# Softmax of the cross attention: one exponential for eight heads instead of eight

## The chip, the cores and the metric

The kernel runs on one core of a Trainium2 chip. The time is the device time of one launch, in microseconds (us). Before the change it is 1782.53 us, the median of three runs (1781.92 to 1785.18).

A core has five engines that run side by side, each with its own queue in order: TensorE (PE; PEld is its loading of weights), VectorE (DVE), ScalarE (ACT), GpSimd (POOL) and SyncE (SP, which only issues transfers here). TensorE writes to PSUM, the other engines compute from PSUM or SBUF; POOL works in SBUF alone. In the profile an instruction stands under the line of the kernel that issued it (L359 is line 359).

## The reference

The program is a decoder of two layers on an input of 16 x 128 x 256 floats (16 sequences of 128 tokens of 256 numbers), each block followed by a layer norm: an attention with a causal mask, a gated ensemble, a mixture of experts, then an attention with a band mask, a cross attention with a second input `ctx_512`, and again experts. The change touches the cross attention of the second layer alone, which has 16 heads of 16 numbers and no mask:

```
qh = (q @ Wq + bq).reshape(B, LQ, HEADS, D_K).transpose(0, 2, 1, 3)
kh = (k @ Wk + bk).reshape(B, LKV, HEADS, D_K).transpose(0, 2, 1, 3)
scores = jnp.einsum('bhqd,bhkd->bhqk', qh, kh) * scale
attn = jax.nn.softmax(scores, axis=-1)
out = jnp.einsum('bhqk,bhkd->bhqd', attn, vh)
```

So for every sequence and head there are 128 x 128 scores, and each row of 128 keys is turned into weights: the row's maximum is subtracted, the exponential taken, and the result divided by its sum.

## The kernel before

**Tiles and stages.** The 16 sequences are worked on in four groups of four. A group passes through the six blocks in order; each block is a Python generator that issues a few instructions and then yields an estimate of the time they take. A small weaver merges two such streams into one program: attention blocks as the main stream, and the dense blocks (ensemble and experts) of other groups as the side stream, by given ratios. So while one group's cross attention runs, matrix products of another group's dense block run in between. For the four groups the merging ends in these calls: cross attention (block 4) of group 0 and of group 1 each behind its own band attention (block 3), and groups 2 and 3 in one stretch, each beside the dense stream.

**The order on the engines.** The program's order is not quite that of the queues. The framework below places the instructions of each engine by their order in the text among those that it reckons ready, from its own estimates of durations; a few places are fixed by hand (`together`, `joined`, `keep_in_program_order`).

**Cross attention.** `cross1` projects queries, keys and values, then calls `attention16`, which the band attention calls too. It goes through eight units, one for each sequence of the group and each half of the heads (eight heads a unit). For a unit:

1. POOL writes the keys of four heads side by side, masked by head (`kb`, L493).
2. TensorE makes the scores of eight heads, 128 x 1024 numbers, in two banks of PSUM (tile `psS`, four matmuls of 64 rows, issued through L52). `psS` has one buffer, so the next unit's scores can't be written before all readers of this one are done.
3. `softmax`. For the attentions with a mask, DVE first copies the scores to SBUF with the mask (L349, tile `e`); the cross attention has no mask, `seen` is `None`, and the scores stay in PSUM. DVE reduces each row to its negated maximum (L354, `nmax`, eight numbers a row). ACT then runs one exponential a head, with that maximum as its bias, and gives the row's total with it (L359; the total is a second record, ACTIVATION_READ_ACCUMULATOR). DVE takes the reciprocal of the totals (L364), and POOL multiplies the weights by it (L365).
4. Two units later TensorE transposes the weights (L57, into `psO`), ACT copies them to SBUF (L374, `eT`), TensorE multiplies them with the values (L52), ACT and DVE pick the heads' rows (L528, L531), and the output product is added to the input (L290) and normed.

**The dense work beside it.** Beside group 0's cross attention runs the ensemble: TensorE's hidden rows are finished by DVE (L803). Beside groups 2 and 3 run the experts of the second layer, whose hidden rows are finished by ACT with Gelu (L1213); Gelu and the exponential lie in different function tables, so ACT loads a table (ACT_TABLE_LOAD) at each change between them. Beside group 1 the routed experts of the first layer end, with gathers from memory whose results DVE adds (L292), and the second layer's experts begin. In these dense blocks DVE also builds sums of the hidden rows (L687 to L690) and adds products to accumulators (L709, L711).

Of the kernel before, what the change touches and what calls it, by code (L numbers as in the profile page):

```python
# [10 lines left out]
AF = mybir.ActivationFunctionType  # L11
ALU = mybir.AluOpType
AX = mybir.AxisListType

P = 128
# [14 lines left out]
def kernel(ctx: ExitStack, tc: tile.TileContext, a: dict, out: bass.AP):  # L30
    nc = tc.nc
# [311 lines left out]
    def softmax(s, seen):  # L343

        n = 2 * s.shape[2]
        e = p3.tile([P, n, P], F32, tag="p", name="e")
        scores = e.rearrange("p (s h) k -> p s h k", s=2)
        if seen is not None:
            nc.vector.tensor_tensor(  # L349
                scores, s, seen.unsqueeze(1).unsqueeze(1).to_broadcast([P, 2, n // 2, P]), ALU.min  # L350
            )
            s = scores
        nmax = sp.tile([P, n], F32, tag="nmax", name="nmax")
        nc.vector.tensor_reduce(  # L354
            nmax.rearrange("p (s h) -> p s h", s=2), s, AX.X, ALU.max, negate=True
        )
        total = sp.tile([P, n], F32, tag="total", name="total")
        for h in range(n):
            nc.scalar.activation(  # L359
                e[:, h, :], s[:, h // (n // 2), h % (n // 2), :],  # L360
                AF.Exp, bias=nmax[:, h:h + 1], accum_out=total[:, h:h + 1],
            )
        inv = sp.tile([P, n], F32, tag="inv", name="inv")
        nc.vector.reciprocal(inv, total)  # L364
        nc.gpsimd.tensor_tensor(e, e, inv.unsqueeze(2).to_broadcast([P, n, P]), ALU.mult)  # L365
        return e
# [13 lines left out]
    def attention0(x, g):  # L380
# [24 lines left out]
        def scores(j, b):  # L405
            qT, kT, _, _ = heads0[g, j]
            at = slice(b * P, (b + 1) * P)
            s = ps.tile([P, 2, T], F32, tag="S", name="psS", bufs=1)[:, :, :D].rearrange(
                "p s (i k) -> p s i k", i=2
            )  # L410

            for i in range(2):
                for k in range(2):
                    rows = slice(64 * k, 64 * k + 64)
                    with joined(i == k == 0):
                        mm(
                            s[:, k, i, :], lhsT=qT[rows, i, at], rhs=kT[rows, i, at],
                            start=True, stop=True,
                        )
            return softmax(s, causal)  # L420
# [63 lines left out]
    def attention16(x, qT, kT, v, bv, wo, bo, seen):  # L484
# [3 lines left out]
        def scores(b, c):  # L488

            at = slice(b * P, (b + 1) * P)  # L490

            kb = p2.tile([P, 4, P], F32, tag="kb", name="kb")
            nc.gpsimd.tensor_tensor(  # L493
                kb, kT[:, c, at].unsqueeze(1).to_broadcast([P, 4, P]),
                hm4.unsqueeze(2).to_broadcast([P, 4, P]), ALU.mult,
            )
            yield UNTIL, weaver.now + 2.0
            s = ps.tile([P, 2, T], F32, tag="S", name="psS", bufs=1)
            for k in range(2):
                rows = slice(64 * k, 64 * k + 64)  # L500
                with joined(k == 0):
                    mm(
                        s[:, k, :], lhsT=qT[rows, c, at],
                        rhs=kb[rows].rearrange("p h k -> p (h k)"), start=True, stop=True,
                    )
            return softmax(s.rearrange("p s (h k) -> p s h k", h=4), seen)
# [878 lines left out]
```

## Time and profile before

| | us |
|---|---|
| median of three runs | 1782.53 |
| profiled execution | 1784.85 |
| its span | 1783.2 |
| PE busy | 1677.6 |
| PE weight loads busy | 1037.5 |
| DVE busy | 1051.0 |
| ACT busy | 714.5 |
| POOL busy | 491.4 |
| L359 from PSUM, 256 exponentials (cross attention) | 90.3 |
| L359 from SBUF, 512 exponentials (the other two attentions) | 198.6 |
| L354 from PSUM, 32 reductions | 39.1 |

The profile is of one execution; its own time is a little over its span, which runs from the first to the last instruction. A busy time is the union of an engine's instructions. A row of a group reads: line, engine, operation, output<-inputs, shapes, count, then busy us, mean ns of one, and the idle time of the engine just before these instructions with what ended it. In a row of stretches the columns are the stretch, its length, the busy us (and instructions) of PE, PEld, DVE, ACT and POOL, the granted TensorE clock, and the use of the transfer engines. In a row in order of time they are the start in us, the length, the engine and the instruction. The chain is followed back from the last instruction: at each step to what released it.

### The profile page before, as it was taken

The page shows a single profiled execution, that of the slowest core. Times are in us where ns is not written, and L with a number is a line of the kernel's source. Part 1 is how long each engine was busy: PE and PEld are TensorE (multiplying, and loading weights), DVE is VectorE, ACT ScalarE, POOL GpSimd, SP SyncE. Part 2 cuts the span into 40 slices and gives each one's busy share as a digit, 9 for nine tenths or more (in the row PEclk, how much of TensorE's full clock was granted, in tenths as well). Part 3 has the DMA queues.
Part 4 walks back from the last instruction along what each step waited for, and adds up shares of the span by engine and source line. Part 5 has one row for each costly group of instructions (what it writes and reads, how often), then busy time and mean ns, then how long its engine had stood idle before and what let it go on. Part 6 is the DMA issues. An engine that isn't in the chain of part 4 may idle for free.

```text
span 1783.2 us, 22203 instructions
## 1 busy us (share of the span) xinstructions
PE 1677.6 (94%) x7644; PEld 1037.5 (58%) x7644; DVE 1051.0 (59%) x2129; ACT 714.5 (40%) x2238; POOL 491.4 (28%) x492
## 2 busy tenths in 40 slices
PE   9999999999998999999999779799999999999996
PEld 5656556666665666555556446456555555556664
DVE  4565565576667437777665844475665466545544
ACT  4535311111123340143340634653948687493220
POOL 5311223210002404232320442564533132220000
PEclk9999999999999999999999889899999999999998
DMA  8321233432320496322222028522241202112330
GB/s 270 119 72 43 97 128 120 152 101 103 116 72 28 152 307 223 118 84 85 93 77 95 13 79 287 189 86 112 89 145 57 86 33 86 65 69 86 109 118 33
DMA packets 96706, 195.97 MB, mean 110 GB/s; under 512 B 15961, under 2 KB 58001, under 8 KB 96529
## 3 DMA queue, kind: packets, MB, share of 16 engines
q1 hardware_dynamic: 90688, 171.01, 28.5%
q0 software_dynamic: 5904, 23.54, 3.7%
q8 instruction: 61, 1.00, 0.2%
q14 instruction: 53, 0.43, 0.1%
HBM read 165.09 MB, written 37.81 MB: 114 GB/s over the span
## 4 chain that ended last, share of the span: by engine, by line
PE 71%; DVE 11%; ACT 9%; POOL 3%; issue 2%; DMA 2%; SPq 0%; POOLq 0%; DVEq 0%; ACTq 0%
PE psH L52 40%; PE psM L52 19%; ACT e L359 5%; PE psS L52 4%; PE psO L57 3%; PE psO L52 3%; PE psH L57 2%; DVE nmax L354 1%; ACT L359 1%; DVE x L310 1%; DVE e L349 1%; ACT h L1213 1%; POOL rstd L308 1%; ACT L1213 1%; POOL copies L979 1%
## 5 line engine op out<-in xcount | busy, mean ns | idle before, releaser
L52 PE MATMUL psH<-xT,we 128*128 128x512 f32 x1024 | 496.2, 607 | 9.8 <-ACT h L1213 4.6
L365 POOL TENSOR_TENSOR e<-e,inv 128x512 f32<-128x512 f32 (+1 forms) x128 | 190.1, 1486 | 510.6 <-DVE inv L364 453.3
L52 PEld LDWEIGHTS psH<-xT,we 128*128 128x128 f32 x1024 | 187.3, 192 | 176.1 <-issue 141.3
L359 ACT ACTIVATE e<-e,nmax 128x128 f32<-128x128 f32 x512 | 198.6, 389 | 186.3 <-DVE nmax L354 165.2
L52 PE MATMUL psM<-cm,wb 128*128 128x256 f32 x1024 | 264.4, 383 | 1.5 <-DVE acc L711 1.5
L52 PEld LDWEIGHTS psM<-cm,wb 128*128 128x128 f32 x1024 | 192.6, 191 | 70.2 <-issue 45.1
L711 DVE TENSOR_TENSOR acc<-psM,acc 128x512 f32<-128x512 f32 (+1 forms) x216 | 135.7, 629 | 154.1 <-PE psM L52 153.2
L52 PE MATMUL psM<-h,wb 128*128 128x256 f32 x768 | 201.3, 384 | 1.6 <-ACT h L1213 1.6
L374 ACT COPY eT<-psO 128x512 f32<-128x512 f32 x192 | 107.3, 589 | 224.8 <-PE psO L57 224.3
L52 PEld LDWEIGHTS psM<-h,wb 128*128 128x128 f32 x768 | 142.2, 190 | 65.3 <-issue 44.7
L1213 ACT ACTIVATE h<-psH,b 128x512 f32<-128x512 f32 x128 | 87.1, 688 | 176.0 <-PE psH L52 175.4
L803 DVE SCALAR_TENSOR_TENSOR h<-psH,gt 128x512 f32<-128x512 f32 x128 | 87.9, 687 | 88.9 <-PE psH L52 88.7
L57 PE MATMUL psO<-ident,e 128*128 128x128 f32 x768 | 117.8, 283 | 16.7 <-DVE zT L531 11.9
L57 PEld LDWEIGHTS psO<-ident,e 128*128 128x128 f32 x768 | 89.5, 144 | 68.2 <-issue 33.7
L52 PE MATMUL psH<-xT,wquad 128*128 128x512 f32 x256 | 118.0, 602 | 3.8 <-DMA wquad<-in_L_attn_W_Q 2.9
L493 POOL TENSOR_TENSOR kb<-kT,hm 128x512 f32<-128x512 f32 x64 | 70.7, 1106 | 128.3 <-PE psS L52 72.6
L359 ACT ACTIVATE e<-psS,nmax 128x128 f32<-128x128 f32 x256 | 90.3, 380 | 18.0 <-DVE nmax L354 17.6
L359 ACT ACTIVATION_READ_ACCUMULATOR e<-e,nmax 128x1 f32 x512 | 95.9, 187 | 0.0
L52 PE MATMUL psO<-eT,v 128*64 128x128 f32 (+1 forms) x1024 | 84.0, 345 | 8.0 <-ACT eT L374 8.0
L308 POOL TENSOR_TENSOR rstd<-ve,mhalf 128x4 f32<-128x4 f32 (+1 forms) x32 | 28.6, 893 | 200.3 <-DVE ve L306 200.1
L354 DVE TENSOR_REDUCE nmax<-e 128x4 f32<-128x512 f32 (+1 forms) x96 | 82.5, 859 | 1.9
L52 PE MATMUL psS<-kb,qT 64*128 64x512 f32 x256 | 73.3, 649 | 10.5 <-ACT e L359 5.9
(211 smaller groups left out, 2260.2 us busy)
## 6 DMA issues: line engine op xcount, KB each, us to landing
wb<-wbd SPq DMA_DIRECT2D x48, 896.0 KB
we<-in_L_xattn_proj_in SPq DMA_DIRECT2D x32, 512.0 KB
wt<-table SPq DMA_DIRECT2D x64, 256.0 KB
we<-in_L_ffn_w SPq DMA_DIRECT2D x32, 512.0 KB
wbd<-wb POOLq DMA_DIRECT2D x16, 896.0 KB, 3.9
gt<-gatesd SPq DMA_DIRECT2D x32, 256.0 KB
results<-y SPq DMA_DIRECT2D x10, 768.0 KB
rows<-copies SPq DMA_DIRECT2D x6, 1024.0 KB
```

The costliest lines, as they stand in the source:

```text
L52: recent[0] = nc.tensor.matmul(*args, **how)
L57: return nc.tensor.transpose(out_, in_, ident[:n, :n])
L308: nc.gpsimd.tensor_tensor(rstd[:, at], ve[:, at], mhalf[:, at], ALU.pow)
L310: nc.vector.tensor_scalar(self.x[:, b, :], self.x[:, b, :], self.mv[:, b, 0:1], rstd[:, b:b + 1], ALU.subtract, ALU.mult,)
L354: nc.vector.tensor_reduce(nmax.rearrange("p (s h) -> p s h", s=2), s, AX.X, ALU.max, negate=True)
L359: nc.scalar.activation(e[:, h, :], s[:, h // (n // 2), h % (n // 2), :], AF.Exp, bias=nmax[:, h:h + 1], accum_out=total[:, h:h + 1],)
L365: nc.gpsimd.tensor_tensor(e, e, inv.unsqueeze(2).to_broadcast([P, n, P]), ALU.mult)
L374: return eT, nc.scalar.copy(eT, pt)
L493: nc.gpsimd.tensor_tensor(kb, kT[:, c, at].unsqueeze(1).to_broadcast([P, 4, P]), hm4.unsqueeze(2).to_broadcast([P, 4, P]), ALU.mult,)
L711: nc.vector.tensor_tensor(to, pm[:, :len(slots), :], to, ALU.add)
L803: nc.vector.scalar_tensor_tensor(out=h, in0=ph, scalar=0.0, in1=up[1], op0=ALU.max, op1=ALU.mult)
L1213: nc.scalar.activation(h, ph, AF.Gelu, bias=b1[:, 4 * e + c:4 * e + c + 1])
```

## The change

In `softmax`, when there is no mask (`seen is None`, the cross attention alone), DVE adds the negated maxima of all eight heads to the scores in one operation that reads PSUM and writes the tile `e` in SBUF; ACT takes one exponential over all 1024 numbers of a row, in place; and DVE sums the eight totals in one reduction. With a mask everything stays.

```diff
         total = sp.tile([P, n], F32, tag="total", name="total")
-        for h in range(n):
-            nc.scalar.activation(
-                e[:, h, :], s[:, h // (n // 2), h % (n // 2), :],
-                AF.Exp, bias=nmax[:, h:h + 1], accum_out=total[:, h:h + 1],
-            )
+        if seen is None:
+
+            nc.vector.tensor_tensor(
+                scores, s, nmax.rearrange("p (s h) -> p s h", s=2).unsqueeze(3).to_broadcast(
+                    [P, 2, n // 2, P]
+                ), ALU.add,
+            )
+            nc.scalar.activation(e, e, AF.Exp)
+            nc.vector.tensor_reduce(total, e, AX.X, ALU.add)
+        else:
+            for h in range(n):
+                nc.scalar.activation(
+                    e[:, h, :], s[:, h // (n // 2), h % (n // 2), :],
+                    AF.Exp, bias=nmax[:, h:h + 1], accum_out=total[:, h:h + 1],
+                )
         inv = sp.tile([P, n], F32, tag="inv", name="inv")
         nc.vector.reciprocal(inv, total)
```

## The prediction

> **What bounds the kernel now.** I read the page first (engine shares, chain), then looked for the stages in which the changed lines run, then the busy time, the waits and the order of time in those stages alone.
>
> ```profile
> PE 1677.6 (94%) x7644; PEld 1037.5 (58%) x7644; DVE 1051.0 (59%) x2129; ACT 714.5 (40%) x2238; POOL 491.4 (28%) x492
> ...
> PE 71%; DVE 11%; ACT 9%; POOL 3%; issue 2%; DMA 2%; SPq 0%; POOLq 0%; DVEq 0%; ACTq 0%
> ```
>
> Over the whole span TensorE is the bound, and ACT and DVE have room. But cross attention runs in four stretches only, one per group, eight units each: about 866 to 926 us (A), 1104 to 1185 (B), 1341 to 1403 (C), 1542 to 1605 (D). The busy time of the engines there (PE, PEld, DVE, ACT, POOL, then granted clock and DMA), and in three stretches for comparison:
>
> ```profile
> 866.00:926.00 60.00, 58.10 (x258) 33.26 (x257) 37.28 (x60) 31.14 (x145) 20.50 (x14) 1.00 0.21 70
> 1104.00:1185.00 81.00, 64.37 (x330) 36.26 (x331) 42.88 (x88) 57.14 (x194) 45.41 (x46) 0.92 0.45 147
> 1341.00:1403.00 62.00, 60.51 (x264) 34.18 (x264) 30.38 (x51) 57.51 (x172) 19.35 (x14) 1.00 0.19 64
> 1542.00:1605.00 63.00, 59.06 (x255) 32.57 (x254) 30.35 (x49) 57.42 (x171) 20.24 (x14) 1.00 0.22 78
> 690.00:750.00 60.00, 56.65 (x218) 35.79 (x216) 46.17 (x104) 2.93 (x5) 13.23 (x11) 1.00 0.38 131
> 700.00:720.00 20.00, 18.52 (x83) 12.68 (x84) 18.44 (x46) 1.08 (x2) 4.16 (x3) 1.00 0.39 125
> 830.00:860.00 30.00, 29.17 (x135) 17.34 (x134) 25.23 (x72) 4.20 (x9) 5.45 (x4) 1.00 0.28 88
> ```
>
> In C and D ACT is busy 93% and 91%, DVE 49% and 48%; in A it is the reverse, DVE 62% and ACT 52%. The chain of D, by line:
>
> ```profile
> by line: ACT e L359 28.8%; ACT L359 12.2%; PE psH L52 11.6%; ACT L1213 11.2%; PE psM L52 6.8%; ACT h L1213 6.8%; ACT eT L374 6.7%; issue 6.4%; PE psS L52 3.4%; ACT hz L528 2.0%; DVE nmax L354 1.8%; PE psO L52 1.7%; DVE cm L687 1.1%; ACTq L3
> ```
>
> The exponentials hold 28.8% of D (18.1 us); the same answer gives 18.1% of C (11.2 us), 11.9% of B (9.6 us) and 9.3% of A (5.6 us). One unit of C in order of time, engine by engine, shows why (TensorE, then DVE, then ACT):
>
> ```profile
> 1362.65 1.13 PE L52 MATMUL psS<-kb,qT 64*128 64x512 f32 x4
> ...
> 1370.25 1.13 PE L52 MATMUL psS<-kb,qT 64*128 64x512 f32 x4
> ```
> ```profile
> 1363.83 1.23 DVE L354 TENSOR_REDUCE nmax<-psS 128x8 f32<-128x1024 f32 x1 [1.55 <-PE psS L52]
> ```
> ```profile
> 1365.50 1.28 ACT L359 ACT_TABLE_LOAD   x1
> 1366.80 0.37 ACT L359 ACTIVATE e<-psS,nmax 128x128 f32<-128x128 f32 x1
> ...
> 1369.21 0.40 ACT L359 ACTIVATE e<-psS,nmax 128x128 f32<-128x128 f32 x1
> ```
>
> The score tile psS has one buffer. It is held from the matmul (1362.65) through the reduction, ACT's other work, a table load and eight exponentials (to 1369.61), and the next scores go out at 1370.25: 7.6 us a unit, of which ACT holds 4.5.
>
> **The change part by part.** Per unit (32 of them):
> - Removed: eight exponentials with their totals. From the first start to the last end they take 1366.80 to 1369.61, 2.8 us, and 2.9 with the last total: 32 x 2.9 = 93 us of ACT.
> - Added on DVE: the subtraction, 1024 wide from PSUM, and the sum, 1024 wide from SBUF. Both have a row of the same shape:
>
> ```profile
> L354 DVE TENSOR_REDUCE nmax<-e 128x8 f32<-128x1024 f32 x32 | 38.8, 1213 | 0.5
> L349 DVE TENSOR_TENSOR e<-psS,band 128x1024 f32<-128x1024 f32 x32 | 38.8, 1211 | 6.3 <-PE psS L52 5.6 <-PE psO L57 0.6
> ```
>
>  1.21 + 1.21 = 2.42 us, 32 x 2.42 = 77 us of DVE. Neither row stretches beside POOL (maxima 1226 and 1220 ns; the two-input SBUF form of line 687 reaches 2337 against a median of 692).
> - Added on ACT: one exponential of 1024 from SBUF, of which the trace has no row. The two exponentials without bias from SBUF are:
>
> ```profile
> L848 ACT ACTIVATE r_p<-r_p 128x64 f32<-128x64 f32 x4 | 1.0, 256 | 11.3 <-DVE r_p L847 11.3
> L1194 ACT ACTIVATE g_l<-g_l 128x32 f32<-128x32 f32 x4 | 0.9, 229 | 7.6 <-DVE g_l L1193 7.6
> ```
>
>  27 ns for 32 elements is 0.84 ns each: 256 + 960 x 0.84 = 1.06 us. Two tanh from PSUM (128: 284 ns, 512: 592 ns) give 1.0. I take 1.05; ACT saves 1.85 a unit, 59 us in all.
> - Moved: psS is free after the subtraction, not after the exponentials. The hold becomes 1.13 + 1.23 + 1.21 and some 0.2 of handing on, 3.8 us against 5.5 where ACT is idle (A) and 7.6 (C). The table load is no longer inside it. Loads stay about as many: each unit still sits between Gelus. No DMA is issued or moved. The reciprocal and POOL's multiplication (1.9 us) stay.
> - New wait: the sum waits for ACT on DVE's queue where the reciprocal waited (9.8 us in C, 10.8 in D, 6.0 in B, 1.5 in A). Behind it stand the sums of the accumulators, the halves of Strassen's operands and, in A, the hidden rows. I cost it at nothing more, since ACT's part before it gets shorter by 1.85 a unit; if ACT is late all the same, the wait stands, and the rival below prices that.
>
> What this is worth, stage by stage. The load moves 19.4 us of DVE into each stage and takes 14.8 of ACT out of it.
> - C and D: ACT falls to 42.7 and 42.6 us (69%), DVE rises to 49.8 (80%). What is late next is TensorE's own queue. Its room: weight loads fill 55% of C and 52% of D, but 57.8% of 830 to 860, where DVE is 84% busy, and 59.7% of 690 to 750, where DVE is 77%. At 57.8%, C needs 34.18/0.578 = 59.1 us (-2.9) and D 56.3 (-6.7); at 59.7%, 57.3 (-4.7) and 54.6 (-8.4). I take the first, the row whose DVE is fullest, and in D only -5, because 25% of D's chain is table loads for Gelu, Gelu and copies that stay. C -3, D -5. At the other end, nothing.
> - B: the first units wait openly for the exponentials. The whole share on the chain is 9.6/2.85 = 3.4 units, each 2.85 - 1.21 = 1.64 us shorter: -5.6. From 1150 on DVE is busy 31.55 of 40 us and the chain goes through it (line 292), so three units of 2.42 add up to 7.3 there. I take half of that against it, -1.5; bounds -5.6 and +7.3.
> - A: DVE rises from 37.3 to 56.7 us of 60. The fullest stretch, 700 to 720, holds 92%: 56.7/0.92 = 61.6, +1.6, which I take as nearest to the load; at the 84% of 830 to 860, 67.5, +7.5. Below: two chain units, -3.3.
>
> Sum: 1.6 - 1.5 - 3 - 5 = -7.9 us. The profiled execution took 1784.85 us (span 1783.2 and 1.65 around it), 2.3 above the median of 1782.53; taking the difference off the median, 1774.6.
>
> **The rivals.** 0.2%, 3.6 us, is about what can be told from no change here.
> - TensorE has nothing to give. For it: it is busy 60.51 of 62 us in C. Then only its open waits for the exponentials go (3.5 us in B, 1.0 in C, 1.4 in D), less A's 1.6 and some 2 in B: -2.3, 1780.2. Against it: weight loads at 55% where other stretches reach 60%. On this the Trainium skill (Perfetto Trace Analysis, Identifying the Most-Contended Engine) says that matmul busy time is no measure of TensorE's room and weight-load time is; by that rule this rival falls, and the trace agrees in so far as busy 97% goes with 55% in C and with 57.8% at 830 to 860.
> - DVE becomes the bound (slower). If DVE can hold no more than the 84% of 830 to 860: A +7.5; B from 1150, (31.55 + 7.3)/0.84 = 46.2 of 40, +6.2, less 3.5 before; C and D, 49.8 with the unchanged waits of 9.8 and 10.8 are 96% and gain nothing. +10.2, 1792.7. It passes 3.6 us from a ceiling of about 88% on (A 64.4, +4.4). For it: one in-order queue that waits for ACT; against it: 92% at 700 to 720.
> - The full gain: every exponential on the chain goes and TensorE reaches 59.7%: -3.3 - 5.6 - 4.7 - 8.4 = -22, 1760.5. Against it: DVE at 80% and more.
> - A unit's own chain decides (slower). Reduction to reciprocal takes 1.23 + 2.9 + 0.2 now, then 1.23 + 1.21 + 1.05 + 1.21 + 0.2 with two more handings on of 0.1: +0.7. If transposes waited for it, 32 x 0.7 = 22 us, 1804.9. Against it: TensorE waits for POOL's weights only 0.8 us in C and none in A, where the first unit is multiplied by 873.4 and transposed at 882.4. The Trainium skill (Perfetto Trace Analysis, Optimizing Scalar/DVE Operations) speaks for this one: it says that where ACT or DVE is not saturated, smaller instructions may finish sooner, and ACT in A is at 52%; those 9 us of slack say that here nobody would notice.
> - That the order changes. In the trace DVE runs lines 711 and 803 between lines 354 and 364, which are neighbours in the text, so the order on each queue is made from estimated readiness, and it is made anew. A stall like B's (TensorE waits 8.2 us for zT, and then runs at half clock for 10.2 us, 1148.5 to 1158.8) can come or go, some 5 us either way. It widens the range and is no case of its own.
>
> **How the numbers follow.** Forecast (-4 to -14): 0.37; full gain: 0.10; TensorE has nothing to give: 0.17; DVE the bound: 0.31; a unit's chain: 0.05. Faster 0.47, same 0.17, slower 0.36. The range leaves out the ends of the full gain and most of the last rival: 1762 to 1795; the forecast's own is 1768 to 1779.
>
> **What would show it.** The subtraction and the sum at 1.2 us, the exponential at 1.0 to 1.1; ACT down 59 us, DVE up 77; no wait of psS for ACT at the exponentials; psS to psS down to 7 us in C and D, which get 3 to 5 us shorter; A not shorter, DVE over 90% in it. It is wrong if TensorE in A waits for DVE's hidden rows or accumulators by more than 2 us, if the sum's wait on DVE is as long as the reciprocal's was, or if the exponential costs far more than 1.1 us.

## The result, and the profile after

The median fell from 1784.20 us to 1778.78 us (15 runs each), a ratio of 0.9972 with a 95% interval of 0.9960 to 0.9983: 5 us faster, between 3 and 7. One of the 15 runs after took 3393 us and is left out of the ratio. Measured once more beside the experiments it was 0.9963 (0.9951 to 0.9975), some 6.6 us. The forecast of -7.9 us, 0.9956, had the sign right and the size too large. The profiled execution took 1782.95 us (span 1781.3), only 1.9 us less than the one before. Single executions of one kernel lie up to 10 us apart (1774.26 to 1784.57 after), so the stages below are compared by the same matmuls in both traces, and not by the ends of the spans.

The page after, engine shares and chain:

```profile
PE 1680.1 (94%) x7644; PEld 1041.4 (58%) x7644; DVE 1130.3 (63%) x2193; ACT 659.0 (37%) x1758; POOL 492.0 (28%) x492
...
PE 73%; DVE 14%; ACT 5%; POOL 3%; DMA 2%; issue 2%; POOLq 0%; DVEq 0%; SPq 0%; ACTq 0%
```

DVE has 79 us more (77 were forecast), ACT 55.5 less (59). ACT's share of the chain fell from 9 to 5%, DVE's rose from 11 to 14%. The groups by shape give the three new instructions and the first reduction (line, engine, operation, shapes, count, then busy us, mean ns, idle before):

```profile
L360 DVE TENSOR_TENSOR e<-psS,nmax 128x1024 f32<-128x1024 f32 x32 | 39.0, 1220 | 1.1
L366 DVE TENSOR_REDUCE total<-e 128x8 f32<-128x1024 f32 x32 | 38.9, 1214 | 8.2 <-ACT e L365 8.1
...
L365 ACT ACTIVATE e<-e 128x1024 f32<-128x1024 f32 x32 | 33.8, 1057 | 31.1 <-DVE e L360 30.7
```

1.22, 1.21 and 1.06 us, against 1.21, 1.21 and the 1.05 taken from two rows of other sizes. The sum waits 8.1 us for ACT in the whole program; the reciprocal had waited 9.8 in stage C alone.

The four stretches after (PE, PEld, DVE, ACT, POOL, clock, DMA):

```profile
866.00:929.00 63.00, 60.75 (x261) 34.15 (x260) 55.52 (x74) 16.85 (x25) 20.57 (x13) 0.97 0.21 70
1107.00:1188.00 81.00, 69.30 (x338) 40.14 (x337) 62.21 (x103) 44.62 (x76) 48.05 (x47) 0.91 0.45 148
1344.00:1405.00 61.00, 61.00 (x268) 35.10 (x267) 50.34 (x68) 45.98 (x54) 20.69 (x14) 1.00 0.19 71
1542.00:1603.00 61.00, 59.70 (x264) 34.21 (x263) 52.06 (x67) 45.35 (x54) 21.11 (x14) 1.00 0.19 72
```

In C and D ACT went from 93% and 91% busy to 75% and 74%, DVE from 49% to 83 and 85%. The chain of C, before and then after, shows what took ACT's place (in all rows of this document the line numbers are those of the kernel traced; a row of ACT without a tile is the table load of that line):

```profile
by line: PE psH L52 21.8%; ACT e L359 18.1%; PE psM L52 15.6%; PE psS L52 8.8%; ACT L359 8.3%; ACT L1213 6.2%; ACT h L1213 5.4%; issue 3.7%; ACT eT L374 2.7%; PE psO L57 2.4%; DVE cm L687 2.2%; DVE nmax L354 1.9%; PE psO L52 1.8%; ACT hz L5
```
```profile
by line: PE psH L52 38.7%; PE psM L52 34.1%; PE psS L52 13.9%; PE psO L57 9.3%; PE psO L52 4.7%
```

Nothing but TensorE is left on it: before, the exponentials and the table loads before them stood there with 26%. In D it is not so; subtraction (L360), exponential (L365), Gelu (L1223) and DVE's sums of hidden rows (L699, L700) are on the chain after:

```profile
by line: PE psH L52 20.0%; PE psM L52 15.8%; PE psS L52 7.1%; DVE e L360 5.9%; DVE nmax L354 5.8%; ACT e L365 5.2%; ACT h L1223 4.8%; DVE cm L699 4.7%; DVE cm L700 4.7%; ACT L1223 4.4%; ACT L365 4.2%; PE psO L52 4.0%; issue 3.8%; PE psO L57
```

How long each stage takes can be read from the same matmul in each trace. The table gives, in us, the time from the first scores of a cross attention to a fixed later matmul: for A to C the first scores of the next band attention, for D the 897th of the 1024 hidden-row matmuls of the experts. So each holds the cross attention and the dense work just behind it.

| trace | A | B | C | D |
|---|---|---|---|---|
| before | 117.4 | 135.5 | 88.7 | 117.6 |
| the change | 117.6 | 135.6 | 86.3 | 114.5 |
| the change, second trace | 117.6 | 134.9 | 86.3 | 114.5 |

C gains 2.4 us, D 3.1, B between nothing and 0.6, A loses 0.2: -5.2 to -5.9, in keeping with the 5.0 and 6.6 us of the ratios. The small changes of A and B are hardly clear of what those stages do by themselves: in the traces of kernels that leave the stage as it was, A takes 115.6 to 117.4 and B 135.4 to 136.2. Three of the four traces with the change in group 1 lie just below that for B, at 134.9.

B's small net hides a change of waits. What TensorE waits for before its transposes there, before (stretch 1104 to 1185) and after (1107 to 1188); the columns are us in total, times, longest:

```profile
PE psO L57 <- DVE zT L531: 11.0, 3, 8.2
```
```profile
PE psO L57 <- POOL e L375: 5.6, 3, 2.7
```

The waits for `zT` are gone but for 0.7 us, and those for POOL's weights rose from 0.7 us to 5.6. The other three traces with the change in group 1 show the same (5.7, 5.7 and 6.8 us). Why POOL is late there was not tried.

### The profile page after: what moved, and what is told of

Read it like the earlier page. It is cut to its first block, busy times and chain, and to the rows that moved or that the text cites. A ratio compares the mean times of both kernels' runs of the same rounds, so it can differ in the third digit from the quotient of the medians.

```text
span 1781.3 us, 21784 instructions
## 1 busy us (share of the span) xinstructions
PE 1680.1 (94%) x7644; PEld 1041.4 (58%) x7644; DVE 1130.3 (63%) x2193; ACT 659.0 (37%) x1758; POOL 492.0 (28%) x492
## 4 chain that ended last, share of the span: by engine, by line
PE 73%; DVE 14%; ACT 5%; POOL 3%; DMA 2%; issue 2%; POOLq 0%; DVEq 0%; SPq 0%; ACTq 0%
PE psH L52 40%; PE psM L52 20%; PE psS L52 4%; PE psO L57 4%; PE psO L52 3%; PE psH L57 3%; ACT e L369 2%; DVE nmax L354 2%; DVE x L310 1%; DVE e L349 1%; POOL rstd L308 1%; POOL copies L989 1%; DVE x L292 1%; DVE h L813 1%; DVE acc L721 1%
## 5 line engine op out<-in xcount | busy, mean ns | idle before, releaser
L1223 ACT ACTIVATE h<-psH,b 128x512 f32<-128x512 f32 x128 | 87.5, 688 | 189.5 <-PE psH L52 189.0
L57 PEld LDWEIGHTS psO<-ident,e 128*128 128x128 f32 x768 | 91.1, 146 | 62.3 <-issue 36.1
L52 PEld LDWEIGHTS psH<-xT,wquad 128*128 128x128 f32 x256 | 47.3, 192 | 57.2 <-issue 46.7
```

The lines of the kernel that those rows point to most:

```text
L52: recent[0] = nc.tensor.matmul(*args, **how)
L57: return nc.tensor.transpose(out_, in_, ident[:n, :n])
L1223: nc.scalar.activation(h, ph, AF.Gelu, bias=b1[:, 4 * e + c:4 * e + c + 1])
```

## The experiments

All go by the ratio to the kernel before on the same chip.

**One stage at a time.** The softmax gets an argument that says which form to use, and the cross attention hands it over by group:

```diff
-            return softmax(s.rearrange("p s (h k) -> p s h k", h=4), seen)
+            return softmax(s.rearrange("p s (h k) -> p s h k", h=4), seen, how)
...
-        if seen is None:
+        if how == "one":
```

Group 0 alone:

> The change in the first stage alone (group 0), the other three groups as before. Theory (each stage pays by its own limit: DVE in the first, ACT in the last two): 1 to 4 us slower than before, ratio 1.0005 to 1.0025, because DVE rises there from 37 to 56 us of some 60. Rival (the earlier release of the score tile pays wherever a unit waits for it, DVE has room): 1 to 4 us faster, 0.998 to 0.9995. Rival (the gain of the whole comes from a new order of the queues and not from a stage): anything, and the single stages don't add up to the whole.

Group 1 alone:

> The change in the second stage alone (group 1). Theory: the open waits at its start go, the additions of the gathered rows on DVE are pushed back by the same: within 2 us of before, 0.999 to 1.001. Rival (the stage waits for exponentials): 3 to 6 us faster, 0.9965 to 0.9985. Rival (DVE is the bound there): 3 to 7 us slower.

Groups 2 and 3 alone:

> The change in the last two stages alone (groups 2 and 3, beside the experts with Gelu). Theory: all of the gain and none of the first stage's cost: 5 to 8 us faster than before, 0.9955 to 0.9972, as fast as the whole change or up to 3 us faster. Rival (the gain lies in the first two stages, or in the order): within 2 us of before.

All but group 0:

> The change in all stages but the first. Theory: the whole change without the first stage's 1 to 4 us: 6 to 9 us faster than before, 0.995 to 0.9967. Rival (the first stage gains as well): less gain than the whole change, 2 to 4 us faster.

| the change in | ratio | interval | us | A | B | C | D |
|---|---|---|---|---|---|---|---|
| group 0 | 1.0001 | 0.9989 to 1.0012 | 0 | 117.6 | 136.1 | 88.7 | 117.6 |
| group 1 | 0.9982 | 0.9971 to 0.9993 | -3 | 115.7 | 134.9 | 88.7 | 117.6 |
| groups 2, 3 | 0.9961 | 0.9947 to 0.9975 | -7 | 117.4 | 135.6 | 86.3 | 114.5 |
| groups 1, 2, 3 | 0.9960 | 0.9947 to 0.9973 | -7 | 115.6 | 134.9 | 86.3 | 114.5 |

C and D are independent of the other stages and repeat to a tenth of a microsecond: 86.3 and 114.5 wherever the change is on, 88.7 and 117.6 wherever it is off. Groups 2 and 3 hold all of the gain that the stages' own times show clearly. Group 0 neither gains nor costs, against my 1 to 4 us of loss, and against the rival's gain as well. Group 1 measured 3 us faster, outside the range of my theory and inside that of the first rival, but its own stage only shows 0.6 in the trace; 1.7 us of the difference lie in A, where that kernel has no change at all. That 1.7 is time at half clock and is told of at the end. Over all its runs, too, that kernel had a little more clock (a mean granted clock of 0.9819 in 12 runs, against 0.9810 in the 23 of before); if TensorE is the bound, that is an estimated 1.6 of its 3 us.

The rival that the gain comes from a new order of the queues falls for C and D, whose times do not depend on what the other stages do. In the stage times the single stages add up to the whole. By the ratios they do not: 0, -3 and -7 would be -10, where groups 1, 2 and 3 together gave -7 and the whole change -5.0 and -6.6; the -3 of group 1 is the part that the stage times do not bear out.

**Which half of the mechanism it is.** The change does two things to a unit: it frees the score tile before ACT comes to it, and it takes some 1.85 us a unit off ACT. Two kernels do one each, in groups 2 and 3 alone. The first frees the tile and leaves ACT its eight exponentials with their totals:

```diff
-            nc.scalar.activation(e, e, AF.Exp)
-            nc.vector.tensor_reduce(total, e, AX.X, ALU.add)
+            for h in range(n):
+                nc.scalar.activation(
+                    e[:, h, :], e[:, h, :], AF.Exp, accum_out=total[:, h:h + 1],
+                )
```

> Groups 2 and 3 alone: DVE subtracts the maxima into SBUF as in the change, but ACT still takes eight exponentials with their totals, from SBUF; DVE makes no sum. The score tile is free after the subtraction, ACT keeps about 3 us a unit, DVE gets half of the addition. Theory that the early release of the score tile brings the gain: 5 to 8 us faster than before, as with the whole change in these groups (0.9961). Theory that the relief of ACT (15 of 57 us in each of the two stages) brings it: at most 2 us faster, 0.999 to 1.002.

The second writes the differences back to PSUM, so that one exponential relieves ACT but the tile is held until it is done:

```diff
             nc.vector.tensor_tensor(
-                scores, s, nmax.rearrange("p (s h) -> p s h", s=2).unsqueeze(3).to_broadcast(
+                s, s, nmax.rearrange("p (s h) -> p s h", s=2).unsqueeze(3).to_broadcast(
...
-            nc.scalar.activation(e, e, AF.Exp)
+            nc.scalar.activation(scores, s, AF.Exp)
```

> Groups 2 and 3 alone: the subtraction writes back to the score tile in PSUM, the one exponential reads it there, and the sum is as in the change. ACT and DVE have the loads of the change, but the score tile is held until the exponential is done, with the table load inside. Theory of the early release: most of the gain is gone, within 3 us of before, 0.9985 to 1.0015. Theory of ACT's relief: 5 to 8 us faster, 0.9955 to 0.997.

| | ratio | interval | C | D | tile held, C / D | unit to unit, C / D |
|---|---|---|---|---|---|---|
| before | 1 | | 88.7 | 117.6 | 7.12 / 7.49 | 7.67 / 7.83 |
| the change in groups 2, 3 | 0.9961 | 0.9947 to 0.9975 | 86.3 | 114.5 | 4.36 / 4.85 | 7.32 / 7.18 |
| tile freed, ACT not relieved | 0.9995 | 0.9983 to 1.0008 | 88.8 | 117.1 | 4.40 / 4.44 | 7.53 / 7.52 |
| ACT relieved, tile not freed | 1.0014 | 1.0003 to 1.0025 | 89.4 | 116.9 | 7.36 / 7.11 | 7.61 / 7.86 |

(Held: from the start of a unit's first score matmul to the end of the last reader of the scores, mean of the eight units, in us.) Neither half alone is worth anything that the ratios can tell. Each of the two theories met its range in one of the kernels and missed it in the other, so both fall as I had put them. In D the single traces show 0.5 and 0.7 us for the halves, against 3.1 for both together. The 1.0014 of the second is not seen in its stages, which are 0.0 us in sum against before in its trace; the mean granted clock of its 12 runs is 0.9802, against 0.9820 before, which would be an estimated 3 us. The stretches C and D of the first of the two:

```profile
1337.00:1399.00 62.00, 60.53 (x264) 34.15 (x261) 38.13 (x58) 54.70 (x172) 20.77 (x14) 1.00 0.18 64
1537.00:1600.00 63.00, 60.08 (x261) 33.48 (x260) 40.17 (x59) 54.84 (x173) 20.11 (x14) 1.00 0.19 69
```

ACT is still busy 88 and 87% of the time. No score matmul of C waits for an exponential any more, but TensorE now waits for Gelu's hidden rows: its weight loads stand 3.1 us for them in C and 2.6 in D, against 0.6 and 0.2 before and none with the change. The exponentials (L365) are 11.5% of C's chain and the table loads 12.4%:

```profile
by line: PE psH L52 24.6%; PE psM L52 20.5%; ACT e L365 11.5%; PE psO L57 8.0%; PE psS L52 6.8%; ACT L365 6.2%; ACT L1224 6.2%; PE psO L52 4.6%; ACT h L1224 3.5%; issue 3.1%; DVE e L359 2.0%; DVE nmax L354 1.9%; DVE cm L700 1.1%; DVE cm L70
```

In the second ACT is down to 43 of 62 us in C, yet the tile's loop is as long as before: 1.8 us of exponentials went out of it, 1.2 us of subtraction came in, and the table load is still in it. The waits of its C:

```profile
ACT L364 <- DVE psS L359: 13.2, 6, 3.0
DVE total L365 <- ACT e L364: 6.7, 6, 1.9
...
PE psS L52 <- ACT e L364: 1.2, 2, 0.6
```

ACT idles 13.2 us for the differences, DVE waits 6.7 us for ACT at its sum, and TensorE still waits for the exponential. So the gain comes only when both are moved: that is measured. The reading of it is that the stages had two limits of nearly the same length, ACT's queue (57.5 us of work in C, 7.2 a unit) and the loop through the one score buffer (7.67 us from unit to unit).

**What DVE's time costs.** The same sum made twice, in groups 2 and 3, and then in group 0:

```diff
-            nc.vector.tensor_reduce(total, e, AX.X, ALU.add)
+            for _ in range(2):
+                nc.vector.tensor_reduce(total, e, AX.X, ALU.add)
```

> Groups 2 and 3 alone, with the change, and the sum of DVE made twice: 1.21 us more of DVE a unit, 9.7 us in each of the two stages, where DVE is busy 50 of 61 us with the change. Theory that DVE is the next bound from some 92% on: it would stand at 98%, so 4 to 8 us of the 7 us gain are lost, 0.9985 to 1.001. Theory that DVE still has room: within 2 us of the change in these groups, 0.995 to 0.997.

> Group 0 alone, with the change and the sum of DVE made twice: DVE would have 65 us of work in a stage of 63. Theory that DVE is the limit of the first stage with the change: 5 to 10 us slower than the change in this group alone, 1.003 to 1.0065 against before. Theory that DVE has room there: 0 to 2 us slower, 1.000 to 1.0015.

In groups 2 and 3: 1.0017 (1.0006 to 1.0028), C 88.2, D 119.9. By the ratios the whole gain of 7 us is lost and 3 more, about 10 us for 19.4 us of DVE, where 4 to 8 had been expected. By the stage times it is 7.3 us, 1.9 in C and 5.4 in D. The mean granted clock of its 12 runs is 0.9803, against 0.9820 before, which would be an estimated 3 of the 10 us. C and D there:

```profile
1337.00:1399.00 62.00, 60.94 (x265) 34.46 (x265) 57.88 (x73) 45.63 (x54) 19.87 (x13) 1.00 0.20 66
1537.00:1600.00 63.00, 58.45 (x252) 32.35 (x251) 57.33 (x67) 41.86 (x51) 20.39 (x13) 0.97 0.20 69
```

DVE stands at 93 and 91%, and its added time costs, as expected. In D one open wait of TensorE, for DVE's addition of an output product (L290), accounts for 2.7 of the 5.4 us; with the change alone TensorE does not wait there:

```profile
PE psH L52 <- DVE x L290: 2.7, 1, 2.7
```

Another 1.7 us are a stretch of 3.4 us at half clock, which begins at 1584.2, as that wait ends. In group 0, where I expected a loss all the more: 1.0000 (0.9987 to 1.0012), none at all. Its A takes 115.9 us, 0.2 more than the unchanged first stage where that has no half-clock stretch. A and the 57 us behind it, and after them the same two of before:

```profile
864.00:924.00 60.00, 57.93 (x257) 33.21 (x258) 58.30 (x78) 17.08 (x25) 20.16 (x13) 1.00 0.19 70
924.00:981.00 57.00, 56.37 (x233) 35.80 (x232) 38.17 (x78) 5.51 (x11) 6.25 (x5) 1.00 0.33 104
```
```profile
866.00:926.00 60.00, 58.10 (x258) 33.26 (x257) 37.28 (x60) 31.14 (x145) 20.50 (x14) 1.00 0.21 70
926.00:983.00 57.00, 56.37 (x228) 36.08 (x226) 34.05 (x70) 5.51 (x11) 5.75 (x5) 0.97 0.31 103
```

DVE is 97% busy for 60 us, and TensorE is as busy with loading weights in it (33.2 us, 33.3 before) and in the stretch behind (35.8 against 36.1). What didn't fit was done behind the stage, where DVE had been busy 34 of 57 us and now is 38. So 92%, the ceiling that I had read off one stretch of 20 us, is no ceiling. Nor does DVE's share of the chain tell the two cases apart. C of groups 2 and 3, where it costs, and A of group 0, where it doesn't, both with the sum twice:

```profile
by line: DVE total L366 20.6%; DVE e L359 11.5%; DVE nmax L354 11.0%; PE psH L52 10.3%; DVE cm L698 8.5%; PE psM L52 5.2%; DVE cm L697 5.1%; ACT e L364 3.4%; DVE acc L721 3.3%; DVE cm L699 3.1%; DVE cm L700 3.1%; PE psO L57 2.7%; DVE acc L7
```
```profile
by line: DVE total L366 19.0%; PE psH L52 14.6%; PE psM L52 10.4%; DVE e L359 9.9%; DVE nmax L354 9.4%; DVE h L813 7.1%; PE psS L52 5.3%; DVE acc L721 4.4%; PE psO L57 3.4%; PE psO L52 3.0%; DVE cm L699 2.8%; issue 2.6%; DVE cm L697 2.0%; A
```

DVE holds more than half of both. Room behind the stage is not the difference either: with the change, DVE is busy 61% of the 60 us behind C and 52% of those behind D, and in A's case 60% before. Why C and D do not absorb the addition is settled only for the wait in D. The traces also show that A's DVE waits 0.5 us for the exponential in its 62 us and D's 3.0 in 64, behind table loads that A doesn't have; that this is a cause was not tried.

**The same in the band attention.** Groups 2 and 3, cross attention as in the change, and the band attention too; there the score tile is free after the mask, in both forms:

```diff
-        yield from attention16(x, qT, kT, v, None, wo, bp1, band)
+        yield from attention16(x, qT, kT, v, None, wo, bp1, band, ('heads', 'heads', 'one', 'one')[g])
```

> Groups 2 and 3: the change in the cross attention and the same in the band attention, whose score tile is free after the mask already. ACT is relieved by another 15 us in each of these two stages (it is busy 56 of 60 us there), DVE gets 19 us more (38 of 60 busy). Theory of ACT's relief: 3 to 7 us faster than the change in these groups, 0.992 to 0.9945 against before. Theory of the early release: nothing to gain, and DVE at 95% costs: 0.996 to 1.001.

It measured 0.9976 (0.9965 to 0.9987), within the range of the early release and outside that of ACT's relief. That is some 2.6 us slower than the change in groups 2 and 3 alone, a difference that the two intervals do not clear. From the first scores of group 2's band attention to those of its cross attention it takes 103.3 us instead of 101.9, in group 3 111.7 instead of 112.0. The stretches of group 2, before and with this kernel:

```profile
1239.00:1341.00 102.00, 97.01 (x419) 55.63 (x417) 64.30 (x114) 67.74 (x187) 44.78 (x48) 1.00 0.31 112
```
```profile
1237.00:1340.00 103.00, 97.17 (x416) 55.21 (x416) 84.55 (x131) 54.00 (x69) 48.78 (x47) 1.00 0.31 111
```

ACT loses 13.7 us, DVE gets 20.3, and TensorE stands no better. Here ACT does not hold the score tile, and the exchange of exponentials for DVE's time buys nothing. DVE pays a little more for it than in the cross attention: the subtraction from SBUF to SBUF takes 1.34 us on average, against 1.22 from PSUM.

**Once more, side by side.** The change as it is, and in groups 2 and 3 alone:

> The change as it is, once more, beside the next kernel on the same chip: 0.996 to 0.9985 against before.

> The change in groups 2 and 3 alone, once more. Theory (the first stage costs some 2 us in the trace, the second about as much either way): 0.9945 to 0.9972, 0 to 4 us under the change as it is. Rival (no stage costs anything, the stages only add gains): slower than the change as it is by 1 to 4 us.

0.9963 (0.9951 to 0.9975) and 0.9964 (0.9950 to 0.9977). There is no difference to be told. No mix of the stages that was measured beats the change as it is.

## Why the prediction was right, and where its sizes were off

- **What holds psS.** Right, and shown. The hold fell from 7.12 to 4.35 us in C and from 7.49 to 4.85 in D (3.8 had been reckoned without waits on DVE's queue). The table load left the loop; there are 78 loads in the program before and after, as said.
- **The prices.** 77 us of DVE forecast, 79 measured; 59 us of ACT forecast, 55.5 measured. The exponential, worked out from rows of 32 and 64 elements, was right to 0.01 us.
- **C and D, -3 and -5.** The mechanism was right and the sizes too large: -2.4 and -3.1. The cap was the step that held in C: weight loads fill 57.5% of it after (35.10 of 61; 58.3% in the trace of groups 2 and 3 alone), where 57.8% from the stretch of 830 to 860 had been taken. In D, at 56.1%, the cap was not reached, and its -5 is the term furthest off. I had thought of its Gelus and table loads and taken off too little for them: they and DVE are still on D's chain.
- **A, +1.6.** The mis-sized term on the other side: +0.2 in the traces, and nothing to be told from 0 by the ratio. The step that failed is dividing DVE's work by a ceiling inside the stage's bounds: with the sum twice DVE went to 97% there at no cost. A stage is not closed; some of DVE's work went into the stretch behind, where DVE was 60% busy. TensorE waits nowhere in A for DVE's hidden rows or accumulators, which was to be the sign of being wrong.
- **B, -1.5.** Between +0.1 and -0.6, where B varies by 0.8 without any change. The -1.5 does not follow from its own terms: half of 7.3 against -5.6 is -1.95, and the sum would then be -8.4. The open waits of the scores for exponentials (3.5 us) went as said. What came in their place was not in the sum: the stall for `zT`, which the prediction had as able to come or go, went, and waits for POOL's weights came. That these cancel so nearly is luck.
- **The sum.** -7.9 forecast, -5.2 to -5.9 by stages, -5.0 and -6.6 by the ratios. That it came out within the forecast's -4 to -14 owes something to luck: the errors of D (+1.9) and A (-1.4) partly cancel, and 1778.78 us is at the slow end of 1768 to 1779.
- **The rivals.** That TensorE has nothing to give would have been -2.3: its count of open waits is what the change beats in C (1.0 us of open waits for the exponentials, 2.4 us gained), though C was 97.6% busy. By the rule of the Trainium skill (Perfetto Trace Analysis, Identifying the Most-Contended Engine) that matmul busy time does not show the room, the rival had to fall, and the trace agrees: weight loads went from 55.1 to 57.5% of C. That DVE becomes the bound was close: the change leaves DVE at 83 to 85% in C and D, and 9.7 us more in each took all of the gain. A unit's own chain did not show in C, where TensorE waits for POOL's weights nowhere, nor in A, and in D only with 0.8 us for their loads; in B TensorE does wait for POOL's weights, 5.6 us, but the stage is no longer for it. The full gain of 22 us was not there, since TensorE was the next bound in C at once.

## What to carry to other kernels

When two limits of a stage are nearly equally long, an experiment that moves one of them can show nothing, and so can one that moves the other; look for both in the chain before either is called harmless. Moving work from a saturated engine to one at half load is worth what the next queue leaves over, here 2.4 and 3.1 us in two stages, and in C the weight-load share of a stretch with the new mix was a good cap for it. A busy share alone does not say what added time will cost: DVE at 97% cost nothing in A, and at 93 and 91% it cost all of the gain in C and D, though it had room behind all three. What the trace can name is the instruction of TensorE that comes to wait, as for `x` in D.

## What was not expected of the hardware

In the 117 us of stage A there is a half-clock stretch of 3.4 us in some executions and not in others, and the stage takes 1.7 us longer with it. Where the first stage is as before, it begins between 956 and 961 us in five traces, which take 117.3 to 117.4 us, and is missing in four others, which take 115.6 to 115.7. So 1.7 us of a difference between two single executions can be this alone; the group 1 kernel's seeming gain in A is that. In the three traces with the change in group 0 it begins between 905 and 911, within a microsecond of the end of a gap of 2.2 us in TensorE's work; that gap is 1.5 us before the change and 1.4 with the sum made twice, and there no stretch begins with it. The stretches at 956 to 961 have no gap of more than 0.35 us just before them. What sets them off was not tried.
